# Third graph layer: float32r products of split operands in place of f32 products, one buffer of sums

## The chip, the cores and the metric

The kernel runs on one core of a Trainium2 chip. The metric is the device time of one execution in microseconds (us). The engines are TensorE (PE; its weight loads are PEld), VectorE (DVE), ScalarE (ACT), GpSimd (POOL) and SyncE (SP, which here only issues DMAs).

## The reference

The network has four blocks over 512 nodes of 768 features. Each block adds a graph layer and a token mixer to the residual, then a feed-forward part. The change is in the graph layer of the third block (`L2_gnn` in the reference), a relational graph convolution applied three times. `src`, `dst` and the edge types (four of them) describe 8704 edges.

```python
def _rgcn_conv(x, weight, root, bias, src, dst, etype):
    n = x.shape[0]
    out = x @ root + bias
    for r in range(NUM_REL):
        sel = etype == r
        self_f = sel.astype(x.dtype)
        deg = jnp.zeros((n,), x.dtype).at[dst].add(self_f)
        norm = jnp.where(sel, 1.0 / jnp.maximum(deg[dst], 1.0), 0.0)
        h_r = x @ weight[r]
        msgs = h_r[src] * norm[:, None]
        out = out + jax.ops.segment_sum(msgs, dst, num_segments=n)
    return out
x = jax.nn.relu(_rgcn_conv(entity, W1, root1, b1, src, dst, edge_type))
x = jax.nn.relu(_rgcn_conv(x, W2, root2, b2, src, dst, edge_type))
x = _rgcn_conv(x, W3, root3, b3, src, dst, edge_type)
```

Each application thus has five products of 768 by 768 weights (the root and four types) over 512 nodes.

## The kernel before

All four blocks are one program. The kernel is written in a layer that records tiles and instructions in the order of the Python code and then plans each engine's queue itself: an instruction goes into its engine's queue when the plan has its inputs and a buffer ready, and of several that are ready the one that was written earlier goes first. `issue_after` pins an order where the author wants one; nothing in the changed stage is pinned. Each engine then works through its queue in order, and semaphores hold it where an input or a buffer is not there yet.

The changed stage is `gnn2` (L1617), which follows the mixer `mix2` and precedes the feed-forward part of the third block. A register read earlier (`self.wrong`) chooses one of two bodies. The second, with `small` true, is the one that runs. In it the edges have become a dense matrix of small whole numbers, `C`: for each of the four types, how many edges lead from one node to another. The matrix lies in DRAM as `S32`, and four transfers with four conversions on ScalarE (L1634, L1635) bring it into SBUF as float32r.

Node features exist in two layouts. `xn` has nodes on the partitions, four tiles of 128; `xnT` has features on the partitions, six blocks of 128 (`KC`) by 512 nodes. For the sums over edges the features are held as two float32r parts, `parts` (the rounded value, L1647 on ScalarE, and the rest, L1648 on VectorE), which the function `split` makes.

`gather(r)` (L1662) makes the sum over the edges of type `r`: for each of six feature blocks it multiplies eight pieces (four node tiles, two parts) with `C` into a PSUM bank, and VectorE scales the bank by `inv`, one over the in-degree, into `aT` (L1669). `aT` has two buffers. `product` (L1654) multiplies a 768 by 768 weight block, brought in two halves through the pool `wp`, with a feature-major operand in f32, 36 matmuls of 128 by 128 by 512, into six PSUM banks `outs` that stay open over the whole layer (L1659). PSUM has eight banks, so two are left for everything else.

The written order of one layer is: product with the root weights on the layer's own features, `gather(0)`, and then for each type `gather(r + 1)` ahead of `product(r)`. At its end ScalarE adds the bias and takes the relu out of the six banks into `new` (L1690), TensorE transposes it in 24 pieces (L379, in `to_tm`), and `split` turns the result into the next layer's `parts`; after the third layer it is added to the residual instead (`add_x`, L451). In the first layer the in-degrees are computed too, by a product of ones with `C` (L1680) and a reciprocal on VectorE (L1682).

The helper `acc` (L358) issues a run of matmuls into one bank, so its line covers most matmuls of the program. `w` (L282) issues a weight transfer on SyncE's queue. The pool `wp` has six buffers of 2304 f32 per partition, and `rowp` has two of its tag `row`.

Of the kernel before, what the change touches and what calls it, by code (L numbers as in the profile page):

```python
# [10 lines left out]
F32 = mybir.dt.float32  # L11
BF16 = mybir.dt.bfloat16
F32R = mybir.dt.float32r
# [4 lines left out]
OP = mybir.AluOpType  # L18
# [4 lines left out]
P = 128  # L23
# [12 lines left out]
START = BASE * OFF  # L36
MAGIC = 1.5 * 2.0 ** 23
WIN = 40
PER = N * P / NE


# [149 lines left out]
class Net:  # L191
# [1424 lines left out]

    def gnn2(self, xn, xnT):  # L1617
        with self.tc.If(self.wrong > 0) as cmp:
            self.gnn2_with(xn, xnT, False)
        with cmp.Else():  # L1620
            self.gnn2_with(xn, xnT, True)

    def gnn2_with(self, xn, xnT, small):


        nc, tc, d = self.nc, self.tc, self.d
        with ExitStack() as c:
            one = c.enter_context(tc.tile_pool(name="g2_one", bufs=1))
            two = c.enter_context(tc.tile_pool(name="g2_two", bufs=2))
            C = one.tile([P, NT, 4, N], F32R if small else F32, name="C")  # L1630
            for t in range(NT):
                if small:
                    S = two.tile([P, KC, N], F32, name="aT")[:, :4, :]
                    nc.gpsimd.dma_start(S, self.S32[t])  # L1634
                    nc.scalar.copy(C[:, t], S)  # L1635
                else:
                    nc.gpsimd.dma_start(C[:, t], self.S32[t])
            inv = one.tile([P, 4, N], F32, name="inv")
            parts = one.tile([P, NT, 2, D], F32R, name="parts") if small else None
            ones = self.ones  # L1640
            if small:
                ones = one.tile([P, P], F32R, name="onesr")
                nc.scalar.copy(ones, self.ones)

            def split(t, nb, v):
                at = slice(nb * HW, (nb + 1) * HW)
                nc.scalar.copy(parts[:, t, 0, at], v)  # L1647
                nc.vector.tensor_sub(parts[:, t, 1, at], v, parts[:, t, 0, at].bitcast(F32))  # L1648

            h, hT = xn, xnT  # L1650
            for l in range(3):
                outs = [self.ps() for _ in range(KC)]

                def product(blocks, xT, first, last):  # L1654
                    for nb in range(2):
                        w = self.wk(blocks[nb, 0])
                        for f in range(3):
                            for k in range(KC):
                                nc.tensor.matmul(outs[nb * 3 + f], w[:, k, f * P : (f + 1) * P], xT[:, k, :],  # L1659
                                                 start=first and k == 0, stop=last and k == KC - 1)  # L1660

                def gather(r):  # L1662
                    aT = two.tile([P, KC, N], F32, name="aT")
                    for f in range(KC):
                        p = self.ps()
                        at = slice(f * P, (f + 1) * P)
                        self.acc(p, [(parts[:, t, i, at], C[:, t, r, :]) for t in range(NT) for i in range(2)] if small
                                 else [(h[:, t, at], C[:, t, r, :]) for t in range(NT)])
                        nc.vector.tensor_mul(aT[:, f, :], inv[:, r, :], p)  # L1669
                    return aT  # L1670

                if l == 0 and small:
                    for t in range(NT):
                        for nb in range(2):
                            split(t, nb, xn[:, t, nb * HW : (nb + 1) * HW])
                product(d[f"g2_r{l + 1}"], hT, True, False)
                if l == 0:
                    for r in range(4):
                        p = self.ps()
                        self.acc(p, [(ones, C[:, t, r, :]) for t in range(NT)])  # L1680
                        nc.vector.tensor_scalar(inv[:, r, :], p, 1.0, None, OP.max)  # L1681
                        nc.vector.reciprocal(inv[:, r, :], inv[:, r, :])  # L1682
                held = gather(0)
                for r in range(4):
                    after = gather(r + 1) if r < 3 else None
                    product(d[f"g2_w{l + 1}"][r], held, False, r == 3)
                    held = after
                new = two.tile([P, KC, N], F32, name="new", bufs=1)
                for f in range(KC):
                    nc.scalar.activation(new[:, f, :], outs[f], AF.Relu if l < 2 else AF.Identity,  # L1690
                                         bias=self.col(f"g2_b{l + 1}", f))
                hT = new
                if l == 2:
                    self.to_tm(hT, self.add_x)
                elif small:
                    self.to_tm(hT, split)
                else:
                    self.to_tm(hT, lambda t, nb, p: self.copy(h[:, t, nb * HW : (nb + 1) * HW], p))

# [544 lines left out]
```

## Time and profile before

| what | value |
|---|---|
| median of 3 runs | 3911.43 us (3908.42 to 3917.52) |
| the profiled execution, its own time | 3911.17 us |
| its span | 3909.4 us |
| mean granted TensorE clock | 0.991 |
| `gnn2` on TensorE (first product to last transpose) | 1842.0 to 2457.5 us |
| TensorE busy from 1842.0 to 2052.6 (layer one) | 205.29 of 210.60 us |
| TensorE busy from 2052.6 to 2256.0 (layer two) | 203.37 of 203.40 us |
| TensorE busy from 2256.0 to 2458.0 (layer three) | 201.52 of 202.00 us |

In a group of the page the columns are: line, engine, operation, output and inputs by the program's names, shape, count | busy time, mean nanoseconds of one | idle time before it and what ended that. A timeline line has the start, the busy time and then the same. A line of one source has shortest, median and longest duration in nanoseconds. A window has its length, then the busy time of PE, PEld, DVE, ACT and POOL with the number of instructions, the granted clock, the DMA share and the GB/s. A matmul's duration includes its passage through a pipeline that works on several at once, so the distance from one start to the next is what one costs.

### The profile page before, as it was taken

What the parts mean: (1) busy time and instruction counts of PE and PEld (TensorE: products, weight loads), DVE (VectorE), ACT (ScalarE), POOL (GpSimd) and SP (SyncE); (2) the same over time, 40 slices, a digit from 0 to 9 for tenths busy, and PEclk for the clock granted to TensorE, in tenths of its full rate; (3) what the DMA queues carried; (4) which work ended last, traced back from release to release, by engine and by line L of the source; (5) the groups of instructions that cost most, each with busy time, mean ns of one, the idle gap of its engine ahead of it and who ended that gap; (6) DMA issues with size and microseconds to landing.
All of it is one profiled execution on the core that took longest, in us unless ns stands there. A gap on an engine that the chain in (4) does not pass through costs nothing. (4 is left out here: it accounts for less than half of the span.)

```text
span 3909.4 us, 37247 instructions
## 1 busy us (share of the span) xinstructions
PE 3782.9 (97%) x15163; PEld 2045.8 (52%) x15171; DVE 1143.6 (29%) x2788; ACT 600.5 (15%) x1142; POOL 273.0 (7%) x333
## 2 busy tenths in 40 slices
PE   8999999999999999999999999899999999999998
PEld 5554555544556676546545455555644444444443
DVE  9322111245221565132201010347612212212211
ACT  0320000122222164011000000226300000000000
POOL 2300000100210201000000000211100000000000
PEclk9999999999999999999999999899999999999999
DMA  4201111211820213112111110641599999999998
GB/s 183 110 25 61 60 47 63 77 65 73 335 98 25 85 49 130 37 61 94 59 61 61 61 61 3 255 168 49 232 411 423 424 424 424 424 424 424 424 425 358
DMA packets 96309, 710.78 MB, mean 182 GB/s; under 512 B 11744, under 2 KB 11984, under 8 KB 26496
## 3 DMA queue, kind: packets, MB, share of 16 engines
q1 hardware_dynamic: 75312, 601.27, 38.2%
q0 software_dynamic: 16912, 95.99, 6.4%
q10 hardware_dynamic: 3904, 11.01, 0.7%
q8 instruction: 125, 2.05, 0.2%
q14 instruction: 56, 0.46, 0.0%
HBM read 685.68 MB, written 22.54 MB: 181 GB/s over the span
## 5 line engine op out<-in xcount | busy, mean ns | idle before, releaser
L2064 PE MATMUL ps<-w,xg 128*64 128x384 f32 x3072 | 566.1, 489 | 6.9 <-DMA w<-in_f_Wu_dram 3.5
L2064 PEld LDWEIGHTS ps<-w,xg 128*64 128x64 f32 x3072 | 237.0, 137 | 295.0 <-issue 263.3
L1659 PE MATMUL ps<-aT,w 128*128 128x512 f32 x864 | 372.3, 592 | 0.0
L2080 PE MATMUL ps<-w,hT 128*64 128x384 f32 x1536 | 320.3, 490 | 3.3 <-DMA w<-in_f_Wd_dram 1.9
L358 PE MATMUL ps<-xnT,w 128*128 128x512 f32 x684 | 300.5, 595 | 0.3 <-ACT xnT L276 0.2
L1659 PEld LDWEIGHTS ps<-aT,w 128*128 128x128 f32 x864 | 164.1, 190 | 203.0 <-issue 202.3
L358 PE MATMUL ps<-w,xnT 128*128 128x384 f32 x672 | 223.1, 489 | 0.2 <-DVE xnT L274 0.2
L2080 PEld LDWEIGHTS ps<-w,hT 128*64 128x64 f32 x1536 | 132.7, 137 | 163.6 <-issue 139.1
L358 PEld LDWEIGHTS ps<-xnT,w 128*128 128x128 f32 x684 | 129.5, 191 | 159.1 <-issue 155.7
L451 DVE TENSOR_TENSOR x<-x,ps 128x384 f32<-128x384 f32 x224 | 123.1, 553 | 275.0 <-PE ps L358 205.0
L358 PE MATMUL ps<-w,hT 128*128 128x384 f32 x552 | 184.6, 490 | 2.8 <-ACTq L1114 1.5
L358 PEld LDWEIGHTS ps<-w,xnT 128*128 128x128 f32 x672 | 127.6, 191 | 89.7 <-issue 5.7
L2067 ACT ACTIVATE h<-ps 128x384 f32<-128x384 f32 x64 | 31.4, 490 | 794.2 <-PE ps L2064 794.2
L358 PEld LDWEIGHTS ps<-w,hT 128*128 128x128 f32 x552 | 103.1, 190 | 80.3 <-ACT xbT L276 7.1
L1669 DVE TENSOR_TENSOR aT<-inv,ps 128x512 f32<-128x512 f32 x72 | 49.3, 686 | 322.8 <-PE ps L358 322.8
L358 PE MATMUL ps<-C,parts 128*128 128x512 f32 x576 | 137.7, 399 | 2.6 <-DVE inv L1681 2.1
L2068 DVE TENSOR_TENSOR h<-h,ps 128x384 f32<-128x384 f32 x64 | 35.4, 554 | 355.7 <-PE ps L2064 347.1
L2035 PE MATMUL ps<-xnT,sw 128*128 128x512 f32 x288 | 135.4, 603 | 0.0
L358 PE MATMUL ps<-w,aT 128*128 128x384 f32 x384 | 129.3, 486 | 0.8 <-DVE aT L274 0.6
L358 PE MATMUL ps<-w,nodesT 128*128 128x384 f32 x384 | 129.1, 486 | 0.0
L358 PEld LDWEIGHTS ps<-C,parts 128*128 128x128 f32 x576 | 109.2, 190 | 30.0 <-issue 3.8
L1690 ACT ACTIVATE new<-ps,cols 128x512 f32<-128x512 f32 x18 | 12.4, 687 | 574.7 <-PE ps L1659 574.7
(516 smaller groups left out, 4463.1 us busy)
## 6 DMA issues: line engine op xcount, KB each, us to landing
w<-in_f_Wg_dram SPq DMA_DIRECT2D x128, 1152.0 KB, 22.7
w<-in_f_Wu_dram SPq DMA_DIRECT2D x128, 1152.0 KB, 22.2
w<-in_f_Wd_dram SPq DMA_DIRECT2D x128, 1152.0 KB, 22.2
w<-in_g_w_dram SPq DMA_DIRECT2D x54, 1152.0 KB, 5.1
w<-in_m_wqkv_dram SPq DMA_DIRECT2D x24, 1152.0 KB, 6.4
w<-in_g_t_dram SPq DMA_DIRECT2D x12, 1152.0 KB, 5.1
w<-in_m_wp_dram SPq DMA_DIRECT2D x8, 1152.0 KB, 5.1
ea<-in_attr_dram SPq DMA_DIRECT2D x17, 512.0 KB, 9.8
```

Of the source, the lines that this page charges most:

```text
L358: i = self.nc.tensor.matmul(out, a, b, start=n == 0, stop=n == len(pairs) - 1)
L451: self.nc.vector.tensor_add(xs, xs, p)
L1659: nc.tensor.matmul(outs[nb * 3 + f], w[:, k, f * P : (f + 1) * P], xT[:, k, :], start=first and k == 0, stop=last and k == KC - 1)
L1669: nc.vector.tensor_mul(aT[:, f, :], inv[:, r, :], p)
L1690: nc.scalar.activation(new[:, f, :], outs[f], AF.Relu if l < 2 else AF.Identity, bias=self.col(f"g2_b{l + 1}", f))
L2035: i = nc.tensor.matmul(p, w[:, k, :], xnT[:, k, :], start=k == 0, stop=k == KC - 1)
L2064: nc.tensor.matmul(p[a * 64 : a * 64 + 64, :HW], xg[:, k, a * CAP : (a + 1) * CAP], ws[b][a][:, k, :], start=k == 0, stop=k == KC - 1)
L2067: nc.scalar.activation(h, pg[:, :HW], AF.Silu)
L2068: nc.vector.tensor_mul(h, h, pu[:, :HW])
L2080: nc.tensor.matmul(po[nb][a * 64 : a * 64 + 64, :HW], hT[:, f * P + a * 64 : f * P + a * 64 + 64], wd[a][:, f, nb * HW : (nb + 1) * HW], s ...
```

## The change

The body that runs becomes a function of its own, `gnn2_small`; the other, `gnn2_any`, keeps the old code in f32 and isn't run. Write a value as a sum of a top part of 12 bits and the rest, v = t + l. `operand` makes three float32r tiles of a feature block: the top (ScalarE), 4096 times the rest (GpSimd subtracts in place, ScalarE scales), and the difference of the two (VectorE). `thirds` makes the same of a 128-column slice of the weights: the top (ScalarE), the rest and the top less 4096 times the rest (VectorE). The products of tops and of rests share the open bank, `outs`; the product of the differences goes to a bank of its own and is added, times -1/4096, into `sums`, which lies in the memory of `xn`. At the end of the layer `outs` times 1 + 1/4096 is added to it. So each f32 matmul is replaced by three float32r matmuls, 18 for each of the six output blocks of a product.

The operands lie in `ops`, one buffer instead of the two of `aT`, and a type's product now stands before the next type's gather. The scaled sums pass through `v`, in the two buffers of `row`. Weight halves and slices share `wp`, and the four pieces of the count matrix use `wp` on their way to `C` instead of `aT`. The new features overwrite `xnT`.

```diff
+TIMES = 4096.0
+CUT = 1.0 - 2.0 ** -13
...
+    def cut(self, top, x):
+        self.nc.scalar.activation(top, x, AF.Copy, scale=CUT)
+
+    def thirds(self, w, f):
+        nc = self.nc
+        out = self.wp.tile([P, 3, KC, P], F32R, tag="w", name="w3")
+        top, low, dif = (out[:, i] for i in range(3))
+        w = w[:, :, f * P : (f + 1) * P]
+        self.cut(top, w)
+        nc.vector.tensor_sub(low, w, top.bitcast(F32))
+        nc.vector.scalar_tensor_tensor(dif, low.bitcast(F32), -TIMES, top.bitcast(F32), OP.mult, OP.add)
+        return out
+
+    def gnn2_small(self, xn, xnT):
...
+            C = one.tile([P, NT, 4, N], F32R, name="C")
+            ops = one.tile([P, 3, KC, N], F32R, name="ops")
...
+            for t in range(NT):
+                S = self.wp.tile([P, 4, N], F32, tag="w", name="S")
+                nc.gpsimd.dma_start(S, self.S32[t])
+                nc.scalar.copy(C[:, t], S)
+            nc.scalar.copy(ones, self.ones)
+            sums = xn.rearrange("p t d -> p (t d)").rearrange("p (f n) -> p f n", f=KC)
...
+            def operand(k, v):
+                top, low, dif = (ops[:, i, k, :] for i in range(3))
+                self.cut(top, v)
+                nc.gpsimd.tensor_sub(v, v, top.bitcast(F32))
+                nc.scalar.activation(low, v, AF.Copy, scale=TIMES)
+                nc.vector.tensor_sub(dif, top.bitcast(F32), low.bitcast(F32))
+
+            for l in range(3):
...
+                def sliced():
+                    w = self.wk(blocks[0][0][0, 0])
+                    for i in range(len(blocks)):
+                        for f in range(3):
+                            yield self.thirds(w, f)
+                            if f == 0 and i + 1 < len(blocks):
+                                b, nb = blocks[i + 1]
+                                after = self.wk(b[nb, 0])
+                        w = after
+
+                slices = sliced()
+                ready = [next(slices) for _ in range(2)]
+
+                def product(n):
+                    for o in range(KC):
+                        ready.append(next(slices, None))
+                        w = ready.pop(0)
+                        for i in range(2):
+                            for k in range(KC):
+                                nc.tensor.matmul(outs[o], w[:, i, k], ops[:, i, k, :], start=n == 0 and i + k == 0,
+                                                 stop=n == 4 and i == 1 and k == KC - 1)
+                        p = self.ps()
+                        self.acc(p, [(w[:, 2, k], ops[:, 2, k, :]) for k in range(KC)])
+                        if n:
+                            nc.vector.scalar_tensor_tensor(sums[:, o, :], p, -1.0 / TIMES, sums[:, o, :], OP.mult, OP.add)
+                        else:
+                            nc.vector.tensor_scalar(sums[:, o, :], p, -1.0 / TIMES, None, OP.mult)
+
+                if l == 0:
+                    for t in range(NT):
+                        for nb in range(2):
+                            split(t, nb, xn[:, t, nb * HW : (nb + 1) * HW])
+                for k in range(KC):
+                    operand(k, xnT[:, k, :])
+                product(0)
...
+                for r in range(4):
+                    for f in range(KC):
+                        p = self.ps()
+                        at = slice(f * P, (f + 1) * P)
+                        self.acc(p, [(parts[:, t, i, at], C[:, t, r, :]) for t in range(NT) for i in range(2)])
+                        v = self.rowp.tile([P, N], F32, tag="row", name="v")
+                        nc.vector.tensor_mul(v, inv[:, r, :], p)
+                        operand(f, v)
+                    product(r + 1)
+                for f in range(KC):
+                    nc.vector.scalar_tensor_tensor(sums[:, f, :], outs[f], 1.0 + 1.0 / TIMES, sums[:, f, :], OP.mult, OP.add)
+                    nc.scalar.activation(xnT[:, f, :], sums[:, f, :], AF.Relu if l < 2 else AF.Identity,
+                                         bias=self.col(f"g2_b{l + 1}", f))
+                self.to_tm(xnT, split if l < 2 else self.add_x)
...
-            C = one.tile([P, NT, 4, N], F32R if small else F32, name="C")
...
-                held = gather(0)
-                for r in range(4):
-                    after = gather(r + 1) if r < 3 else None
-                    product(d[f"g2_w{l + 1}"][r], held, False, r == 3)
-                    held = after
```

More of the change, by code (lines that the diff above doesn't have):

```diff
@@ L1618, in gnn2 @@
         with self.tc.If(self.wrong > 0) as cmp:
-            self.gnn2_with(xn, xnT, False)
+            self.gnn2_any(xn, xnT)
         with cmp.Else():
-            self.gnn2_with(xn, xnT, True)
-    def gnn2_with(self, xn, xnT, small):
+            self.gnn2_small(xn, xnT)
+    def cut(self, top, x):
[9 more added lines that the diff above has]
+        return out
@@ new lines, in gnn2_small, with split @@
+    def gnn2_small(self, xn, xnT):
+        nc, tc, d = self.nc, self.tc, self.d
+        with ExitStack() as c:
+            one = c.enter_context(tc.tile_pool(name="g2_one", bufs=1))
+            C = one.tile([P, NT, 4, N], F32R, name="C")
+            ops = one.tile([P, 3, KC, N], F32R, name="ops")
+            inv = one.tile([P, 4, N], F32, name="inv")
+            parts = one.tile([P, NT, 2, D], F32R, name="parts")
+            ones = one.tile([P, P], F32R, name="onesr")
+            for t in range(NT):
[4 more added lines that the diff above has]
+            sums = xn.rearrange("p t d -> p (t d)").rearrange("p (f n) -> p f n", f=KC)
+            def split(t, nb, v):
+                at = slice(nb * HW, (nb + 1) * HW)
+                nc.scalar.copy(parts[:, t, 0, at], v)
+                nc.vector.tensor_sub(parts[:, t, 1, at], v, parts[:, t, 0, at].bitcast(F32))
+            def operand(k, v):
[5 more added lines that the diff above has]
+            for l in range(3):
+                blocks = [(b, nb) for b in [d[f"g2_r{l + 1}"]] + [d[f"g2_w{l + 1}"][r] for r in range(4)] for nb in range(2)]
+                outs = [self.ps() for _ in range(KC)]
+                def sliced():
[30 more added lines that the diff above has]
+                product(0)
+                if l == 0:
+                    for r in range(4):
+                        p = self.ps()
+                        self.acc(p, [(ones, C[:, t, r, :]) for t in range(NT)])
+                        nc.vector.tensor_scalar(inv[:, r, :], p, 1.0, None, OP.max)
+                        nc.vector.reciprocal(inv[:, r, :], inv[:, r, :])
+                for r in range(4):
+                    for f in range(KC):
+                        p = self.ps()
+                        at = slice(f * P, (f + 1) * P)
[9 more added lines that the diff above has]
+                self.to_tm(xnT, split if l < 2 else self.add_x)
@@ L1626, in gnn2_with, with gnn2_any @@
+    def gnn2_any(self, xn, xnT):
         nc, tc, d = self.nc, self.tc, self.d
@@ L1629, in gnn2_with @@
             two = c.enter_context(tc.tile_pool(name="g2_two", bufs=2))
-            C = one.tile([P, NT, 4, N], F32R if small else F32, name="C")
+            C = one.tile([P, NT, 4, N], F32, name="C")
             for t in range(NT):
[L1632 to L1637, printed above, removed]
-            inv = one.tile([P, 4, N], F32, name="inv")
[L1639 to L1648, printed above, removed]
+                nc.gpsimd.dma_start(C[:, t], self.S32[t])
+            inv = one.tile([P, 4, N], F32, name="inv")
             h, hT = xn, xnT
@@ L1666, in gather @@
                         at = slice(f * P, (f + 1) * P)
-                        self.acc(p, [(parts[:, t, i, at], C[:, t, r, :]) for t in range(NT) for i in range(2)] if small
-                                 else [(h[:, t, at], C[:, t, r, :]) for t in range(NT)])
+                        self.acc(p, [(h[:, t, at], C[:, t, r, :]) for t in range(NT)])
                         nc.vector.tensor_mul(aT[:, f, :], inv[:, r, :], p)
                     return aT
[L1672 to L1675, printed above, removed]
                 product(d[f"g2_r{l + 1}"], hT, True, False)
@@ L1679, in gnn2_with @@
                         p = self.ps()
-                        self.acc(p, [(ones, C[:, t, r, :]) for t in range(NT)])
+                        self.acc(p, [(self.ones, C[:, t, r, :]) for t in range(NT)])
                         nc.vector.tensor_scalar(inv[:, r, :], p, 1.0, None, OP.max)
@@ L1694, in gnn2_with @@
                     self.to_tm(hT, self.add_x)
-                elif small:
-                    self.to_tm(hT, split)
                 else:
```

## The prediction

> **What bounds the kernel now.** I read the page first, then the windows over the changed stage, then its timeline by engine, and last single lines for prices. The page says that TensorE is busy for 97% of the span, and its groups hold the two kinds of matmul of this stage:
>
> ```profile
> PE 3782.9 (97%) x15163; PEld 2045.8 (52%) x15171; DVE 1143.6 (29%) x2788; ACT 600.5 (15%) x1142; POOL 273.0 (7%) x333
> L1659 PE MATMUL ps<-aT,w 128*128 128x512 f32 x864 | 372.3, 592 | 0.0
> L358 PE MATMUL ps<-C,parts 128*128 128x512 f32 x576 | 137.7, 399 | 2.6 <-DVE inv L1681 2.1 <-DVE aT L1669 0.5
> ```
>
> An f32 matmul leaves two records: 12 products by 36 are 432 matmuls, and the first group counts 864. A float32r matmul leaves one (3 layers by 4 types by 48 is 576). The mean of one overlaps its neighbours, so the price is the pitch, and TensorE's timeline gives it.
>
> ```profile
> 1907.16 31.06 PE L1659 MATMUL ps<-aT,w 128*128 128x512 f32 x72
> 1937.66 11.48 PE L358 MATMUL ps<-C,parts 128*128 128x512 f32 x48
> 1948.97 31.06 PE L1659 MATMUL ps<-aT,w 128*128 128x512 f32 x72
> 2052.58 3.02 PE L379 MATMUL ps<-ident,new 128*128 128x128 f32 x24
> 2055.44 31.07 PE L1659 MATMUL ps<-new,w 128*128 128x512 f32 x72
> ```
>
> Product follows gather without a gap, and layer two begins as soon as the 24 transposes are over. L1659's weight loads start every 0.429 us (1906.94 is followed by 1907.59, 1908.02, 1908.45), so an f32 matmul costs 0.858 and a product 30.87 us. VectorE's timeline shows a sum over edges every 1.813 us, which is 8 float32r matmuls, so one costs 0.2267:
>
> ```profile
> 2088.38 0.69 DVE L1669 TENSOR_TENSOR aT<-inv,ps 128x512 f32<-128x512 f32 x1 [30.63 <-PE ps L358]
> 2090.19 0.69 DVE L1669 TENSOR_TENSOR aT<-inv,ps 128x512 f32<-128x512 f32 x1 [1.12 <-PE ps L358]
> ```
>
> The stage (1842.0 to 2457.5) is thus TensorE alone, with one exception in layer one: while the reciprocals run on VectorE, the two free PSUM banks wait for them. The first gather then runs at 3.62/8 = 0.45 us per matmul, and the windows show a clock of 0.60.
>
> ```profile
> 1878.00 1.22 DVE L1681 TENSOR_SCALAR inv<-ps 128x512 f32<-128x512 f32 x2
> 1879.14 6.55 DVE L1682 RECIPROCAL inv<-inv 128x512 f32<-128x512 f32 x2
> 1880.56 3.62 PE L358 MATMUL ps<-C,parts 128*128 128x512 f32 x8
> 1880.00:1886.00 6.00, 4.18 (x10) 2.68 (x9) 6.00 (x3) 0.00 (x0) 0.00 (x0) 0.60 0.00 0
> ```
>
> The first two lines also show that the written order isn't the queue's: two clampings in a row stand before two reciprocals, though the loop alternates. The order is planned by readiness.
>
> **The change part by part.**
>
> *Matmuls.* 15 products of 36 f32 matmuls at 0.858 are 463.1 us. 15 products of 108 float32r matmuls at 0.2267 are 367.2, since each has its own weight load as in the gather. That is -95.9 us on the path.
>
> *Weights (`thirds`, 90 of them).* Each is a cut on ScalarE over 768 elements and two VectorE operations over 768. ScalarE: the 384-wide cast L1647 takes 0.506 and the 2048-wide L1635 takes 1.898, a slope of 0.837 ns, so 768 take 0.83 and 512 take 0.61. VectorE: L1354, two SBUF inputs of 768, 0.96 each. With the evacuation of the third product (128x512 from PSUM, 0.69 as L1669) a step costs VectorE 2.61 us beside 18 x 0.2267 = 4.08 of TensorE: hidden, and GpSimd rests there. Weight transfers land in 5.1 us and a block serves three steps (12.2 us), hidden too. Were VectorE's work uncovered at the first steps of a layer, where nothing is cut ahead, a step would cost 0.83 + 1.92 = 2.75 us of latency; that is inside the start and boundary terms below.
>
> *Operands (`operand`, 90 of them).* ScalarE cut 0.61, GpSimd subtraction, ScalarE scaling 0.61, VectorE difference 0.69. The price of the GpSimd step beside VectorE comes from these:
>
> ```profile
> L524 POOL TENSOR_TENSOR S<-S x4: 1259/1263/1267, 105.8 to 138.2; 128x512 f32<-128x512 f32 x4
> 2705.11 8.42 POOL L1744 TENSOR_TENSOR qk<-qk 128x512 f32<-128x512 f32 x5 [0.63 <-DVE qk L1743]
> 2703.27 7.45 DVE L1743 SCALAR_TENSOR_TENSOR qk<-qk,f 128x512 f32<-128x512 f32 x5
> ```
>
> GpSimd alone takes 1.26; beside VectorE operations with two SBUF inputs a pair takes 8.42/5 = 1.68, both engines being stretched. In a gather the difference of one feature block falls beside the subtraction of the next, so the pitch lies between TensorE's 1.81 and 1.68 + 0.69 = 2.37 (pair, then the scaling L1669 behind it). The two buffers of `v` allow (0.69 + 0.61 + 1.68 + 0.61 + hops of 0.04)/2 = 1.9. Weight pieces planned into VectorE's gaps push further. I take 2.05, near the middle of 1.81 and 2.37: 72 x 0.24 = +17 us (0 to 40). [...]
>
> *From gather to product.* `ops` has one buffer, so a product starts when its own gather is through; before, `gather(r + 1)` stood in between. After the last gather matmul: scaling 0.69, cut 0.61 (top ready at 1.4), subtraction 1.26, scaling 0.61 (low at 3.3), difference 0.69 (at 4.1). Step 0 reads the first five tops in 1.1 us, waits 0.3, reads low parts until about 2.8, waits 0.7, and meets the last difference in time. That is 1.0 us, 12 times: +12 (0 if other steps' matmuls are planned into it, 30 with a stretched GpSimd). In the other direction nothing is late: the next gather needs only `parts`, `C` and a bank.
>
> *Layer boundaries (2).* New on the path after the last matmul: evacuation 0.69, sum with `outs` 0.69, activation 0.71. The GpSimd subtraction overwrites `xnT`, so it waits for the transposes, and six in a row take 7.6 (10.3 at 1.71); then scaling and difference: 10.4 to 13.1 us from the last matmul, with 8 `split` copies (0.5 each) queued on ScalarE as well. TensorE has transposes (3.0) and step 0 (4.1) for it, so 3.3 to 6 are lost, and 1.8 for the slow clock (8 x (0.45 - 0.227), as at 1880.56). I take 7 each: +14 (0, if two gathers and other steps fill it, to 20). The clock's row: an idle stretch of 2.73 us, ended at 1878.69, was enough for half speed. [...]
>
> *Start.* The four 1.9 us conversions of `C`, the weight cuts (1.7), 8 copies (4.0) and 12 operand passes (7.3) now stand on ScalarE before the first product is fed; before, it began at once. From 13 us without the conversions to 21 with them, less 4.1 for step 0, are lost, plus the slow clock. Against it, layer one lost 9.1 us before (210.6 from 1841.97 to 2052.58, less 5 x 30.87, 4 x 10.88 and 16 x 0.2267), and the reciprocals can now run inside the wait. Net +10 (0 to 20).
>
> *End.* Evacuation and sum before the last activation: +1.4. `aT` is gone and L1690 stays, now from SBUF. The f32 branch isn't run.
>
> Sum: -95.9 + 17 + 12 + 14 + 10 + 1.4 = -41.5. The profiled execution took 3911.17 us (span 3909.4), 0.3 from the median 3911.43, so I predict 3870. The ends of the terms give -94.5 (all waits nothing) and +15.5 (40, 30, 20 and 20).
>
> **The rivals.** *The waits are filled.* Order by readiness moves first passes of other steps and two gathers into every wait; only 10 for the gathers, 10 for the start and the end are left: -95.9 + 10 + 10 + 1.4 = -74.5, or 3837. For it speaks the reordering above; against it that only two banks and one `ops` are free.
>
> *ScalarE's queue closes a ring (slower).* If low(f) is planned before cut(f + 1), the next subtraction waits for cut, subtraction, scaling: 0.61 + 1.26 + 0.61 + 0.1 = 2.6 per block, 3.05 at 1.71. The two become ready almost together (low at 1.30 + 1.26 = 2.56 after the scaling starts, the next cut at 1.81 + 0.69 = 2.50), so a plan can fall either way. Against my 2.05 that is +40 to +72, or 3910 to 3942. It decides from the point where -41.5 + 72 x (pitch - 2.05) is zero: a pitch of 2.63.
>
> *VectorE's queue closes it.* With the difference always ahead of the next scaling, a block costs the whole loop, 0.69 + 0.61 + 1.26 + 0.61 + 0.69 + 0.2 = 4.1: +148, or 4018. The planned order above speaks against it. That the change isn't run can be excluded: the stage's rows are those of `parts`, the small branch.
>
> **How the numbers follow.** The measurement can tell about 0.2%, 7.8 us. The forecast has 0.52 (0.48 faster by more, 0.02 within, 0.02 slower, from its upper ends), the filled waits 0.12, ScalarE's ring 0.28 (0.02 faster, 0.08 within, 0.18 slower), VectorE's ring 0.08 (slower). Faster is 0.62, within 0.10, slower 0.28. The range from 3832 to 3940 leaves out VectorE's ring, a part of the filled case and the top of ScalarE's ring; the forecast's own is 3840 to 3900.
>
> **What would show it.** Right: 108 float32r matmuls per product at 0.227 us, 24.5 per product; gather blocks near 2.05; about 1 us of TensorE idle before each product, 7 at each boundary; GpSimd at 1.3 to 1.7 per subtraction. Wrong: a product pitch far above 0.227, a gather pitch of 2.6 or more with VectorE waiting for ScalarE, or TensorE waiting inside products for `w3`.

## The result: 0.25% slower

| what | before | after |
|---|---|---|
| median of 11 runs | 3912.63 us (3907.57 to 3919.70) | 3922.53 us (3917.37 to 3929.50) |
| ratio after/before | | 1.0025 (95%: 1.0016 to 1.0034) |
| the profiled execution, its own time | 3911.17 us | 3919.67 us |
| its span | 3909.4 us | 3917.9 us |
| mean granted TensorE clock | 0.991 | 0.983 |

The change was forecast to save 41.5 us and cost 8.5 in the profiled execution. The page of the kernel after shows TensorE with less work in a longer span (before: 3782.9 us, 97%), and two groups of the page say where to look. Columns are those of the page before.

```profile
PE 3735.0 (95%) x15711; PEld 2155.6 (55%) x15711; DVE 1450.7 (37%) x3166; ACT 780.6 (20%) x1412; POOL 392.1 (10%) x423
L1705 PE MATMUL ps<-ops,w 128*128 128x512 f32 x1080 | 293.0, 417 | 47.6 <-ACT ops L1627 33.8
L1676 POOL TENSOR_TENSOR v<-v,ops 128x512 f32<-128x512 f32 x72 | 92.7, 1287 | 421.3 <-ACT ops L1627 421.3
```

The product's matmuls (L1705, with the third product of differences under L360) were idle for 33.8 us until `cut` (L1627, ScalarE) had written another block of `ops`. GpSimd's subtraction (L1676) took 1.29 us, close to the 1.26 of GpSimd alone, so it was not stretched in the gathers. TensorE's timeline of one type, from gather to gather, places the idle time:

```profile
1933.66 9.26 PE L360 MATMUL ps<-C,parts 128*128 128x512 f32 x40
1943.10 2.11 PE L360 MATMUL ps<-C,parts 128*128 128x512 f32 x8 [0.18 <-DVE v L1733]
1945.05 1.09 PE L1705 MATMUL ps<-ops,w 128*128 128x512 f32 x4
1947.39 0.50 PE L1705 MATMUL ps<-ops,w 128*128 128x512 f32 x1 [1.25 <-ACT ops L1627]
1947.73 0.63 PE L360 MATMUL ps<-ops,w 128*128 128x512 f32 x2
1949.93 3.36 PE L1705 MATMUL ps<-ops,w 128*128 128x512 f32 x7 [1.57 <-ACT ops L1627]
...
1959.38 2.96 PE L1705 MATMUL ps<-ops,w 128*128 128x512 f32 x12
1962.18 1.56 PE L360 MATMUL ps<-ops,w 128*128 128x512 f32 x6
1963.58 2.96 PE L1705 MATMUL ps<-ops,w 128*128 128x512 f32 x12
```

The gather runs almost undisturbed (11.39 us instead of 10.88). The product reads four tops, waits 1.25, reads one more, waits 1.57. The seven matmuls from 1949.93 take 3.15 us to the next start, 0.45 each: half speed, at a granted clock of 0.50. From 1959.38 a step of 18 takes 4.20 us. ScalarE's timeline in the same gather shows what the product waits for (L1627 is the cut, L1677 the scaling by 4096 behind GpSimd's subtraction, L1676):

```profile
1938.53 0.63 ACT L1677 ACTIVATE ops<-v 128x512 fp32r<-128x512 f32 x1 [1.40 <-POOL v L1676]
1939.06 0.62 ACT L1627 ACTIVATE ops<-v 128x512 fp32r<-128x512 f32 x1
1941.09 0.63 ACT L1677 ACTIVATE ops<-v 128x512 fp32r<-128x512 f32 x1 [1.41 <-POOL v L1676]
1941.63 0.62 ACT L1627 ACTIVATE ops<-v 128x512 fp32r<-128x512 f32 x1
1943.63 0.63 ACT L1677 ACTIVATE ops<-v 128x512 fp32r<-128x512 f32 x1 [1.39 <-POOL v L1676]
```

Each cut stands behind the scaling of the block before, and each scaling waits 1.4 us for GpSimd. For the last 0.2 to 0.6 us of that wait the input of the next cut is already there (VectorE writes it until 1938.28, GpSimd is done at 1938.50; for the next block 1940.48 and 1941.06). This is the ring that the prediction named as a rival: cut, subtraction, scaling, next cut, a block every 2.55 us (this distance is called the pitch below) against TensorE's 1.81. From the first block to the sixth that is a lag of 5 x 0.74 = 3.7 us. Two PSUM banks let TensorE finish the gather ahead of VectorE (at 1945.05, where VectorE's last scaling by `inv` starts at 1947.46), so most of the lag is paid where the product begins.

I compare lengths of the stage below: from the start of the mixer's last matmul to the first transposes of layer three (before 1841.81 to 2454.52, 612.71 us; after 1840.43 to 2460.71, 620.28). What lies outside this stretch came to 3298 to 3307 us in nine of the ten profiled executions that I compare (3315 in one), though no experiment edits it, so a few us of difference in a whole time are not the stage's.

### The profile page after: what moved, and what is told of

It is laid out like the page before. It is cut to its first block, busy times and chain, and to the rows that moved or that the text cites. A ratio compares the mean times of both kernels' runs of the same rounds, so it can differ in the third digit from the quotient of the medians.

```text
span 3917.9 us, 39310 instructions
## 1 busy us (share of the span) xinstructions
PE 3735.0 (95%) x15711; PEld 2155.6 (55%) x15711; DVE 1450.7 (37%) x3166; ACT 780.6 (20%) x1412; POOL 392.1 (10%) x423
## 4 chain that ended last, share of the span: by engine, by line
PE 72%; DMA 7%; DVE 5%; ACT 3%; POOL 2%; issue 2%; DVEq 0%; POOLq 0%; another core or an unknown queue 0%; ACTq 0%; SPq 0%
PE ps L360 42%; PE ps L2160 10%; PE ps L1705 6%; PE ps L2176 5%; PE ps L2131 3%; PE ps L381 2%; DMA w<-in_f_Wu_dram 2%; DMA w<-in_f_Wd_dram 2%; POOL v L1676 2%; DMA w<-in_f_Wg_dram 2%; PE ps L1490 2%; ACT ops L1627 1%; PE ps L1471 1%; DVE pt L1240 1%; DVE e L1239 1%
## 5 line engine op out<-in xcount | busy, mean ns | idle before, releaser
L1705 PE MATMUL ps<-ops,w 128*128 128x512 f32 x1080 | 293.0, 417 | 47.6 <-ACT ops L1627 33.8
L360 PE MATMUL ps<-xnT,w 128*128 128x512 f32 x684 | 302.2, 598 | 0.2 <-ACT xnT L278 0.2
L1705 PEld LDWEIGHTS ps<-ops,w 128*128 128x128 f32 x1080 | 213.3, 199 | 111.7 <-ACT ops L1627 44.9
L360 PE MATMUL ps<-w,xnT 128*128 128x384 f32 x672 | 221.9, 487 | 0.4 <-DVE xnT L276 0.2
L360 PEld LDWEIGHTS ps<-xnT,w 128*128 128x128 f32 x684 | 130.1, 192 | 159.8 <-issue 156.2
L360 PE MATMUL ps<-w,hT 128*128 128x384 f32 x552 | 184.6, 490 | 2.8 <-ACTq L1116 1.8
L360 PEld LDWEIGHTS ps<-w,xnT 128*128 128x128 f32 x672 | 126.9, 190 | 89.2 <-issue 4.8
L360 PE MATMUL ps<-ops,w 128*128 128x512 f32 x540 | 148.9, 407 | 6.8 <-DVE ops L1678 6.8
L360 PEld LDWEIGHTS ps<-w,hT 128*128 128x128 f32 x552 | 103.1, 190 | 80.3 <-ACT xbT L278 7.1
L360 PE MATMUL ps<-C,parts 128*128 128x512 f32 x576 | 139.6, 399 | 5.0 <-DVE inv L1725 3.1
L1676 POOL TENSOR_TENSOR v<-v,ops 128x512 f32<-128x512 f32 x72 | 92.7, 1287 | 421.3 <-ACT ops L1627 421.3
L360 PE MATMUL ps<-w,aT 128*128 128x384 f32 x384 | 129.3, 486 | 0.8 <-DVE aT L276 0.6
L360 PE MATMUL ps<-w,nodesT 128*128 128x384 f32 x384 | 129.1, 486 | 0.0
L360 PEld LDWEIGHTS ps<-C,parts 128*128 128x128 f32 x576 | 109.1, 191 | 33.7 <-DVE v L1733 6.8
```

The costliest lines, as they stand in the source:

```text
L360: i = self.nc.tensor.matmul(out, a, b, start=n == 0, stop=n == len(pairs) - 1)
L1676: nc.gpsimd.tensor_sub(v, v, top.bitcast(F32))
L1705: nc.tensor.matmul(outs[o], w[:, i, k], ops[:, i, k, :], start=n == 0 and i + k == 0, stop=n == 4 and i == 1 and k == KC - 1)
```

## The experiments

Each ratio is to the runs of before that were taken along with that kernel.

| kernel | median, us | ratio to before (95%) | stage, us |
|---|---|---|---|
| before | 3912.63 | 1 | 612.71 |
| after | 3922.53 | 1.0025 (1.0016 to 1.0034) | 620.28 |
| cut pinned ahead of the scaling | 3900.11 | 0.9969 (0.9956 to 0.9981) | 598.09 |
| gathers without operand passes | 3851.24 | 0.9840 (0.9823 to 0.9856) | 548.98 |
| subtraction on VectorE | 3859.31 | 0.9862 (0.9845 to 0.9879) | 559.93 |
| 4096 moved into the weights | 3879.87 | 0.9918 (0.9901 to 0.9936) | 577.67 |
| the last two together | 3847.18 | 0.9826 (0.9809 to 0.9843) | 542.81 |
| both queues pinned | 3870.54 | 0.9892 (0.9876 to 0.9909) | 564.38 |
| subtraction on VectorE, counts converted in place | 3858.98 | 0.9867 (0.9851 to 0.9884) | 557.66 |
| 4096 in the weights, VectorE, slices moved 32 bytes | 3854.30 | 0.9839 (0.9826 to 0.9852) | 543.49 |

My theory after the result was that ScalarE's order alone makes the loss between gather and product. The rivals were GpSimd's subtraction as such (its length, or its claim on SBUF against VectorE), and losses elsewhere (start, boundaries, matmul rate).

**How much lies in the operand passes of the gathers.** 

```diff
                         nc.vector.tensor_mul(v, inv[:, r, :], p)
-                        operand(f, v)
```

> Leaves out the operand step (cut, subtraction, scaling, difference) in all 12 gathers, so that the products of the four types read the operand of the layer's own features again; sums over edges are still made and scaled. If the operand chain is what is lost between gather and product, 12 times 5.5 us are won, some 64 us, 3858 us, and TensorE runs without a gap from each gather into its product. If the loss is in the matmuls themselves (their rate, the weights' slices), it stays: 3905 us or more.

It took 71.3 us less than after (both medians and stage lengths), and gather and product follow each other every 36.11 us, 10.91 + 25.2. Of the 71.3, 64 are the losses between gather and product counted below. The rest is in layer one, which is 29.4 us shorter though it had only 21.1 of those losses; there products no longer depend on the reciprocals either. The loss is in these passes, not in the matmul rate or the boundaries.

**ScalarE's order.** The cut of block f + 1 is pinned ahead of the scaling of block f (`scaled`, a function of its own, issues scaling and difference); no other operation is changed.

```diff
-                        operand(f, v)
+                        first = self.cut(ops[:, 0, f, :], v)
+                        nc.gpsimd.tensor_sub(v, v, ops[:, 0, f, :].bitcast(F32))
+                        if f:
+                            with tc.issue_after(first.ins):
+                                scaled(f - 1, before)
+                        before = v
+                    scaled(KC - 1, before)
```

> In the gathers, the cut of block f + 1 is put ahead of the scaling of block f in ScalarE's queue; nothing else changes. Theory (ScalarE's ring): in the changed kernel the queue alternates cut and scaling, so each block waits for cut 0.61, GpSimd's subtraction 1.29 and scaling 0.61, a pitch of 2.55 us against 1.81 of the gather on TensorE, and each of the 12 products starts 5.5 us late, idle and slow clock together. With the ring open the pitch falls to about 1.9, the loss per product to 1.0 to 2.0 us: 42 to 54 us less, about 3870 to 3880 us. Rival (one buffer of operands and a chain of four engines are slow in any order): less than 10 us is won, 3912 us or more.

The answer lay between the two: 22 us gained, and 3900 instead of 3870. VectorE's timeline shows that the ring had moved (L1683 is the difference, L1738 the scaling by `inv`), with GpSimd's beside it:

```profile
2097.85 1.29 POOL L1740 TENSOR_TENSOR v<-v,ops 128x512 f32<-128x512 f32 x1 [0.52 <-ACT ops L1627]
2101.02 1.28 POOL L1740 TENSOR_TENSOR v<-v,ops 128x512 f32<-128x512 f32 x1 [1.88 <-ACT ops L1627]
```

```profile
2098.32 1.36 DVE L1683 TENSOR_TENSOR ops<-ops 128x512 fp32r<-128x512 f32 x1 [1.22 <-ACT ops L1682]
2099.61 0.67 DVE L1738 TENSOR_TENSOR v<-inv,ps 128x512 f32<-128x512 f32 x1
2101.50 1.36 DVE L1683 TENSOR_TENSOR ops<-ops 128x512 fp32r<-128x512 f32 x1 [1.22 <-ACT ops L1682]
2102.78 0.67 DVE L1738 TENSOR_TENSOR v<-inv,ps 128x512 f32<-128x512 f32 x1
```

The difference of block f now stands ahead of the scaling by `inv` of block f + 2, and takes 1.36 us instead of 0.69; it starts 0.47 us into a GpSimd subtraction. The block's pitch is 3.17 us, longer than in after. A type still took 39.56 us instead of 41.57: the planner now puts pieces of the product between the last blocks of the gather, each wait is under 0.6 us, and the clock stays at 1.00 over the whole type, where the type shown of after has 0.92. So the order of two queues decides, and this run alone doesn't tell whether GpSimd's step would still be too long in the right order.

**Both queues in order.** In addition, VectorE's scaling of block f is pinned ahead of the difference of block f - 2 (`diff`); GpSimd keeps its subtraction.

```diff
-                        nc.vector.tensor_mul(v, inv[:, r, :], p)
-                        operand(f, v)
+                        scale_v = nc.vector.tensor_mul(v, inv[:, r, :], p)
+                        if f > 1:
+                            with tc.issue_after(scale_v.ins):
+                                diff(f - 2)
+                        first = self.cut(ops[:, 0, f, :], v)
+                        nc.gpsimd.tensor_sub(v, v, ops[:, 0, f, :].bitcast(F32))
+                        if f:
+                            with tc.issue_after(first.ins):
+                                nc.scalar.activation(ops[:, 1, f - 1, :], before, AF.Copy, scale=TIMES)
+                        before = v
+                    nc.scalar.activation(ops[:, 1, KC - 1, :], before, AF.Copy, scale=TIMES)
+                    for f in range(KC - 2, KC):
+                        diff(f)
```

> GpSimd keeps the subtraction, and the order of both queues is pinned: ScalarE's cut of block f + 1 ahead of the scaling of f, VectorE's scaling of block f + 2 ahead of the difference of f. With only ScalarE pinned VectorE's difference stood ahead of the next scaling and the pitch was 3.17 us. Theory (the order of the queues is the cause): pitch 1.9 to 2.1, 3865 to 3880 us. Rival (GpSimd itself is the cause: while it subtracts, VectorE's difference with two SBUF inputs stands still, 1.36 us instead of 0.69, in any order): pitch 2.3 or more, 3890 us or more.

It came out as the order theory had it: 3870.54 us. That this is also the time I had predicted for the change as it was written is chance: the stage is 48.3 us shorter than before's, more than forecast, and the rest of the profiled execution is 8 us longer. GpSimd's timeline:

```profile
2088.76 1.30 POOL L1742 TENSOR_TENSOR v<-v,ops 128x512 f32<-128x512 f32 x1 [0.52 <-ACT ops L1627]
2090.67 1.30 POOL L1742 TENSOR_TENSOR v<-v,ops 128x512 f32<-128x512 f32 x1 [0.61 <-ACT ops L1627]
```

A block every 1.91 us, with the same operations on the same engines as in after. The differences fall mostly into GpSimd's pauses and take 0.76. The stage is 55.9 us shorter than after's (the medians differ by 52.0): the order of the two queues is worth that much, more than the whole difference between after and the forecast.

**GpSimd's step.** The subtraction goes to VectorE, in the planner's own order.

```diff
-                nc.gpsimd.tensor_sub(v, v, top.bitcast(F32))
+                nc.vector.tensor_sub(v, v, top.bitcast(F32))
```

> The operand's subtraction goes from GpSimd to VectorE (0.69 us instead of 1.29). Theory (ring): cut, subtraction and scaling in turn are 0.61 + 0.69 + 0.61 and hops, at most 2.05 us per block instead of 2.55, and the tail after the last block is 0.6 shorter: 3.0 to 4.0 us less per product, 36 to 48 us in all, 3875 to 3887 us. Rival (VectorE is full: scaling, subtraction and difference are 2.07 us per block against 1.81, with weight slices between them): nothing is won, 3915 us or more.

The time was 3859.31, better than expected. The subtraction takes 0.69 us here, and a type takes 36.54 us. For the first four blocks ScalarE's order is that of after, and the ring turns in 2.05 us, as expected; then the planner puts the fifth cut (2087.36) ahead of the fourth block's scaling (2088.02), so that the order has changed in part as well. The stage is 4.5 us shorter than with both queues pinned. Thus a shorter member shortens the ring even in the old order; how much of the gain is the planner's new order, this run doesn't tell.

**One pass less in the chain.** The factor 4096 goes into the weights' low part, where ScalarE has time; the operand needs three passes instead of four, and the subtraction stays on GpSimd.

```diff
-        nc.vector.tensor_sub(low, w, top.bitcast(F32))
-        nc.vector.scalar_tensor_tensor(dif, low.bitcast(F32), -TIMES, top.bitcast(F32), OP.mult, OP.add)
+        nc.vector.tensor_sub(dif, w, top.bitcast(F32))
+        nc.scalar.activation(low, dif.bitcast(F32), AF.Copy, scale=TIMES)
+        nc.vector.tensor_sub(dif, top.bitcast(F32), low.bitcast(F32))
...
-                nc.gpsimd.tensor_sub(v, v, top.bitcast(F32))
-                nc.scalar.activation(low, v, AF.Copy, scale=TIMES)
-                nc.vector.tensor_sub(dif, top.bitcast(F32), low.bitcast(F32))
+                nc.gpsimd.tensor_sub(low, v, top.bitcast(F32))
+                nc.vector.scalar_tensor_tensor(dif, low.bitcast(F32), -TIMES, top.bitcast(F32), OP.mult, OP.add)
```

> The factor 4096 moves from the operand to the weights: GpSimd writes the rest straight into the operand's low part, VectorE makes the difference, and ScalarE scales each weight slice instead (one operation more per slice, 0.83 us, beside a product of 25 us). No scaling stands in ScalarE's queue between two cuts, so no ring; the chain after the last block is 0.69 + 0.61 + 1.3 + 0.69 with no fourth step. Theory: the loss per product falls from 5.5 to about 1.0, and the start is shorter: 50 to 65 us less, 3858 to 3873 us. Rival (GpSimd beside VectorE at 1.7 per block sets the pace, and slices with one step more come late): 3895 us or more.

The result was 7 us above the expected range. Most types take 36.95 us, as expected, though GpSimd's step is now 1.66 beside VectorE. The last gather of layer two, however, reads so:

```profile
2198.28 0.63 PE L1705 MATMUL ps<-ops,w 128*128 128x512 f32 x2
2199.82 3.92 PE L360 MATMUL ps<-C,parts 128*128 128x512 f32 x16 [0.91 <-DVE v L1733]
2204.95 2.11 PE L360 MATMUL ps<-C,parts 128*128 128x512 f32 x8 [1.21 <-DVE v L1733]
...
2210.20 1.90 PE L1705 MATMUL ps<-ops,w 128*128 128x512 f32 x7 [1.51 <-ACT ops L1627]
```

There VectorE's differences, two in 2.38 us beside GpSimd, stand ahead of the scaling that frees a bank, and the type takes 40.6 us (2192.81 to 2233.41). The last type of the other two layers takes the same, so that these three cost 11 us, more than the 7. By the timeline it is VectorE's order again, in the gathers where the planner mixes other work in; no run pins it there.

**The last two together**, with the subtraction on VectorE:

```diff
-                nc.gpsimd.tensor_sub(low, v, top.bitcast(F32))
+                nc.vector.tensor_sub(low, v, top.bitcast(F32))
```

> Both edits at once: the factor 4096 in the weights, and the operand's subtraction on VectorE, which writes the low part itself. The chain after the last block is then scaling, cut, subtraction, difference, 2.7 us, with nothing on GpSimd and one step of ScalarE. Theory (the chain's length is what is left between gather and product; 0.4 us per product in the kernel with the subtraction on VectorE alone): 0 to 8 us under that kernel's 3859 us, 3851 to 3859 us. Rival (slices with three alternating steps come late, as the starts of products in the kernel with only the factor moved may suggest): 3866 us or more.

It is the fastest version, 0.9826 of before. TensorE's timeline from the first gather of layer two shows gather and product with no gap at all, and a boundary that is filled (2043.76 to 2072.12 is 28.36 us for transposes and the first product, 28.2 without any loss):

```profile
2072.12 11.07 PE L360 MATMUL ps<-C,parts 128*128 128x512 f32 x48
2083.03 1.33 PE L1705 MATMUL ps<-ops,w 128*128 128x512 f32 x5
...
2108.22 11.10 PE L360 MATMUL ps<-C,parts 128*128 128x512 f32 x48
```

**The start.** On the version with the subtraction on VectorE, the counts are loaded into `C` itself and converted in place, so that the weight buffers are free for weights.

```diff
-                S = self.wp.tile([P, 4, N], F32, tag="w", name="S")
-                nc.gpsimd.dma_start(S, self.S32[t])
-                nc.scalar.copy(C[:, t], S)
+                nc.gpsimd.dma_start(C[:, t].bitcast(F32), self.S32[t])
+                nc.scalar.copy(C[:, t], C[:, t].bitcast(F32))
```

> The kernel with the subtraction on VectorE, and the counts are brought straight into C and converted in place, so that they take no buffer of the weights' pool at the start. Theory (the first product waits for its weights, since the four pieces of the count matrix and the mixer's two projection blocks hold all six buffers until the mixer ends): the first weights land before the stage begins and the wait of 15.5 us before the first product falls to 5 to 9 us, 6 to 11 us won, 3848 to 3853 us. Rival (ScalarE's list of conversions, copies and operand passes is as long as before): within 3 us of 3859 us.

The rival's number was right. The first matmul came at 1844.90 instead of 1857.18, but then waited in pieces (3.07 us for a cut, 1.67 for a difference, and more) behind ScalarE's four conversions of 1.88 us each. The first product was over at 1880.62 instead of 1884.14, and the stage was 2.3 us shorter, which the time doesn't resolve. The buffers set when the first matmul starts, then; by the timeline it is mostly ScalarE's amount of work (busy almost without a pause from 1841.69 to 1859.59) that sets when the first product ends. No run takes that work away.

**The rate of a product's matmul.** A step of 18 takes 4.20 us, 0.2333 each, where I had 0.2267 from the gather. To separate the operands, five unread runs of 48 float32r matmuls were put at the end of layer three of the version with the subtraction on VectorE, with stationary and moving operand from either place.

```diff
...
+                    if l == 2 and r == 3:
+                        w, i = self.last
+                        for a, b in ((0, 0), (0, 1), (1, 0), (1, 1), (0, 0)):
+                            p = self.ps()
+                            for j in range(48):
+                                k = j % KC
+                                left = w[:, j // KC % 3, k] if a else parts[:, j // 2 % NT, j % 2, k * P : (k + 1) * P]
+                                right = ops[:, j // KC % 3, k, :] if b else C[:, j // 2 % NT, 0, :]
+                                with tc.issue_after(i.ins):
+                                    i = nc.tensor.matmul(p, left, right, start=j == 0, stop=j == 47)
```

> The kernel with the subtraction on VectorE, and behind the last product five runs of 48 float32r matmuls, each into a bank that nobody reads: stationary and moving operand from parts and C, parts and ops, a weight slice and C, a weight slice and ops, parts and C again. In the changed kernel a matmul of a gather costs 0.2267 us and one of a product 0.2333. If the stationary operand's place makes the difference, the third and fourth runs cost 0.2333 (11.2 us) and the others 0.2267 (10.9 us); if the moving one's does, the second and fourth; if neither, all cost the same. The time itself is some 55 us longer and means nothing.

The runs took 10.91, 10.88, 11.20, 11.20 and 10.91 us from start to start (that kernel takes 3920.08 us, one run). The slice of weights as the stationary operand makes the difference; the moving operand makes none. Two kernels then tried the start address, by moving everything in the pool of the weights by 32 bytes per partition: the runs of 48 again, and the fastest version.

```diff
-        self.edge = edge.tile([P, 120], F32, name="edge")
+        self.edge = edge.tile([P, 128], F32, name="edge")
```

> The kernel of the five unread runs of 48 matmuls (stationary operand from the sums or from a slice of weights, moving operand from the counts or from the operand), with the tile ahead of the weight buffers at 128 numbers per partition instead of 120. If the start address is the cause, all five runs take 10.88-10.91 us. If not, the two runs with a slice of weights stay at 11.20 us.

> The kernel with the factor 4096 in the weights' third part and the subtraction on VectorE (3847.2), with one further edit: the tile of sums over edges that lies ahead of the weight buffers on the right side of SBUF gets 128 numbers per partition instead of 120, so that every slice of weights starts 32 bytes elsewhere, on a multiple of 512 bytes counted from the tile before it. Nothing else is changed. If the start address of the stationary operand is what makes a product's matmul 0.233 us and a gather's 0.227, the 15 products lose 15 x 108 x 0.0066 = 10.8 us and the time is 3834-3839, a step of eighteen matmuls 4.08 instead of 4.20. If the cause is another (the slice is written by two engines, its buffer changes, or the order of use), the time stays at 3844-3850 and the step at 4.20.

Nothing moved: 10.88, 10.89, 11.20, 11.20 and 10.89 us (3924.15 us, one run), and 543.49 us of stage instead of 542.81. The 7 us between the times of the two versions (3854.30 and 3847.18) lie outside the stage. A last kernel asked whether it is the place or the sequence of blocks:

```diff
-                        for a, b in ((0, 0), (0, 1), (1, 0), (1, 1), (0, 0)):
+                        for a, b in ((0, 0), (2, 0), (3, 0), (4, 0), (1, 0), (0, 0)):
...
-                                left = w[:, j // KC % 3, k] if a else parts[:, j // 2 % NT, j % 2, k * P : (k + 1) * P]
+                                left = (parts[:, j // 2 % NT, j % 2, k * P : (k + 1) * P], w[:, j // KC % 3, k],
+                                        ops[:, j // KC % 3, k, : P], w[:, 0, 0], parts[:, 0, 0, :P])[a]
```

> Six unread runs of 48 matmuls at the end of the third layer, all with the counts as the moving operand; the stationary operand is in turn the sums' parts (48 blocks in turn), the operand tile (18 blocks in turn), one block of the last slice of weights repeated, one block of the parts repeated, the slice's 18 blocks in turn, and the parts again. If it is the place of the slice, on the right side of SBUF, the two runs with the slice take 11.20 us and the other four 10.88 to 10.91. If it is the way the slice's blocks change, the run that repeats one block of it takes 10.9. If it is which blocks follow each other, not the place, the operand tile, read in the slice's order, takes 11.20 as well.

```profile
2407.34 11.07 PE L1746 MATMUL ps<-C,parts 128*128 128x512 f32 x48
2418.25 11.04 PE L1746 MATMUL ps<-C,ops 128*128 128x512 f32 x48
2429.13 11.36 PE L1746 MATMUL ps<-C,w 128*128 128x512 f32 x48
2440.33 11.07 PE L1746 MATMUL ps<-C,parts 128*128 128x512 f32 x48
2451.24 11.36 PE L1746 MATMUL ps<-C,w 128*128 128x512 f32 x48
2462.44 11.07 PE L1746 MATMUL ps<-C,parts 128*128 128x512 f32 x48
```

From start to start that is 10.91 (the parts), 10.88 (the operand tile in the slice's order), 11.20 (one block of the slice repeated), 10.91 (one block of the parts repeated), 11.20 (the slice's 18 blocks). (The kernel takes 3929.11 us, one run.) Neither the sequence nor a change of block matters: it is the buffer that the stationary operand lies in. The kernel places the weights' pool on the other side of SBUF from `parts` and `ops` (`side="right"`); what about that place costs 0.0066 us per matmul stays open.

## Why the prediction was wrong, step by step

I predicted 3870 us and the profiled execution took 3919.67. The terms, in us, up to the first transposes of the feed-forward part (before 621.62 from the mixer's last matmul, after 630.73, so 9.1 more, where 41.5 less were forecast: a miss of 50.7):

| term | forecast | measured | from |
|---|---|---|---|
| matmuls | -95.9 | -85.1 | step of 18 is 4.20, a product 25.2; 15 x (25.2 - 24.48) = 10.8 |
| gathers, and gather to product | +17 and +12 | +64.2 | eleven types at 41.57 instead of 36.08, and 3.8 in the first product behind a gather |
| boundaries | +14 | +13.3 | 34.33 and 35.40 less 28.2 each |
| start of layer one | +10 | +15.3 | 12.9 idle, 1.6 slow clock, reciprocals 9.9 instead of 9.1 |
| end | +1.4 | +1.5 | transposes to the next ones 10.45 instead of 8.91 |
| sum | -41.5 | +9.2 | |

*The step that failed* is "from gather to product", together with the pitch of 2.05 that it started from. I let cut(f + 1) run while GpSimd subtracts block f, and priced the hand-over by the last block's latency alone, 1.0 us. The planner put every cut behind the scaling of the block before. What I set at 29 us was 64.2: 35.2 more, the largest part of the 50.7. With both queues in the order that I had assumed the two terms come to about 8.6 us (types of 36.8, 0.6 in the first product behind a gather), so the 29 was no good price for that order either. That is close to the rival's own formula with the measured pitch, 72 x (2.55 - 2.05) = 36. The rival's pitch of 2.6 was right within 0.05, its range to 3.05 was not, since GpSimd wasn't stretched in the gathers. Its point of decision, 2.63, was above the measured 2.55: with my other terms the ring alone would have given 41.5 - 36 = 5.5 us of gain. It needed two more errors of size, the matmul's price and the start, to turn the sign.

*Where the rival's loss shows* I had wrong too. I expected the gather to slow down. TensorE's gather lost only 0.5 us of the 5.5 per type; the rest is waits for tops in the first step and the half clock behind them. In the type shown, 2.82 us are waits, and the 36 matmuls from 1945.05 to 1959.38 took 14.33 - 2.82 = 11.51 us instead of 8.40, so 3.1 are clock (this type lost 6.4 us, more than the mean). The window of that stretch has the clock at 0.76:

```profile
1945.00:1959.40 14.40, 11.57 (x38) 8.59 (x38) 5.87 (x8) 3.78 (x6) 3.71 (x3) 0.76 0.01 1
```

*Mis-sized terms.* The matmul's price of 0.2267 was taken from a gather, where the stationary operand comes from `parts`; the product's takes 0.2333 and 10.8 us more. The start cost 5.3 more than I took, inside its range to 20. I had let the reciprocals run inside the wait for the first product; they came behind that product as before, and the first gather lost 9.9 us to them. The eight splits and GpSimd's subtractions met there (the splits took 10.29 us in after and 3.84 where the subtraction is on VectorE), but that is not what the start cost: with the subtraction on VectorE the first product was over 42.81 us after the mixer's last matmul started, in after 39.80. For a boundary the passes that I listed add up to 11.0 to 13.7 us (2.1, then 7.6 or 10.3, 0.6 and 0.7), not 10.4 to 13.1; the 13.3 measured for the two boundaries are close to the 14 I took all the same.

*What held.* The count of 108 matmuls per product, the two boundaries (13.3 for 14), the end, the weights' slices hidden beside the products, and the statement that the plan of ScalarE's queue can fall either way. My 0.52 for the one side rested on a difference of 0.06 us in readiness (2.50 against 2.56), which is no ground for a preference; in the trace the next cut's input was there 0.2 to 0.6 us before the scaling's, and the queue had the scaling first.

*Overlap and clock.* In the gather of after shown above a difference overlapped a GpSimd subtraction by 0.13 us at most (one ran from 1941.76 to 1942.45, GpSimd's next began at 1942.32); it took 0.69 us, the subtractions 1.29. In the run with the pinned cut one fell into a subtraction: it started 0.82 us before GpSimd's end and ended 0.54 after it (2099.68 against 2099.14), 1.36 us in all and 0.15 less than if it had stood still until that end. In the traces of before and after the granted clock is either 1.00 or 0.50, and its changes lie a whole number of 3.41 us apart (in before it was 0.50 from 1877.96 to 1884.78, twice that). Four of these stretches of after (length, TensorE's busy time, the other engines'; the clock stands third from the end):

```profile
1904.44:1907.85 3.41, 2.14 (x10) 1.43 (x8) 2.08 (x4) 1.15 (x2) 2.08 (x2) 1.00 0.00 0
1907.85:1911.27 3.42, 2.06 (x8) 1.04 (x6) 0.69 (x1) 1.50 (x3) 1.78 (x2) 1.00 0.00 0
1945.40:1948.81 3.41, 1.71 (x7) 0.75 (x5) 1.48 (x3) 1.23 (x3) 2.04 (x2) 1.00 0.02 5
1948.81:1952.22 3.41, 2.29 (x5) 1.84 (x6) 0.98 (x2) 1.70 (x3) 1.28 (x1) 0.50 0.00 0
```

In layer one's first product behind a gather, waits of 1.27 and 1.35 us fell into two stretches and the clock stayed at 1.00. In the type shown, the 1.25 us and the start of the 1.57 fell into one, TensorE was busy for 1.71 of its 3.41 us, and the next stretch had half speed (0.50). The wait of 2.73 us in the kernel before left 1.40 us busy of such a stretch (1874.55 to 1877.96), and the next one had 0.50. So of two products with waits of 1.2 to 1.6 us one lost 3.1 us to the clock and the other none; what differs in these rows is where the waits fell. An exact limit doesn't come out: with 4096 in the weights a wait of 3.17 us, ended at 1888.62, was followed by full speed (the eight matmuls from 1889.64 took 2.00 us, where eight took 3.62 at 1880.56 in the kernel before).

## What to carry to other kernels

Where one engine does two passes of the same block with another engine's pass between them, write down the engine's queue block by block before pricing the passes: the order of f + 1's first pass and f's last one decides whether the pitch is the longest pass or the whole ring (2.55 us here in one order and 1.91 in the other), and a sum of pass times doesn't tell which order a planner will choose. Such an order is cheap to pin, but look at every queue on the ring: here breaking it on one engine moved it to the next. And look for the ring's lag where its consumer has no buffer left, not where the ring turns.

## What was unexpected of the hardware

- A float32r matmul of 128x128 by 128x512 takes 0.2267 us with the stationary operand in `parts` or `ops` and 0.2333 with it in a weight buffer, whatever the moving operand and the sequence of blocks (48 of them took 10.88 to 10.91 us and 11.20); with 32 bytes of shift they took 10.88 to 10.89 and 11.20.
- In the traces of before and after the clock's changes lie a whole number of 3.41 us apart. A stretch of that length with TensorE busy for 1.71 us, idle in two pieces, was followed by half speed; two with 2.14 and 2.06 us busy were not.
- In the run with the pinned cut a VectorE subtraction of 0.69 us took 1.36 when it began during a GpSimd subtraction, while GpSimd's kept its 1.29; at the start of the stage, in after, both were stretched (VectorE's eight splits 10.29 instead of 3.84 in the run with the subtraction on VectorE, GpSimd's first step 1.65).
